# Row slot outermost in the 3x3 run's tiles, and the aggregation copied out of PSUM by ScalarE before VectorE adds it

## The chip, the core and the metric

The kernel runs on one core of a Trainium2 chip. The engines of the core work at the same time, each through its own list of instructions in order: PE (TensorE, the matmuls), DVE (VectorE), ACT (ScalarE), POOL (GpSimd) and SP (SyncE, which here only issues DMAs). They wait for one another with semaphores. The metric is the device time of the whole program in microseconds (us), lower is better. The kernel before took 6639.3 us, the median of 3 runs.

## The reference

The input is `x` of shape 8 x 32 x 128 x 128 (batch, channels, rows, columns). Two layers follow one another, each of the form x + layer(group-normalised x).

```python
xb = _patch_match_stack(x)             # per pixel: the 8 best of 25 shifts, 32 channels -> 256
dct = _conv(xb, dct_w, groups=C)
h = relu(_conv(_conv(xb, w1), w2, groups=CK, pad=1))    # 1x1 over 256 channels, then 3x3 per channel
h = relu(_conv(_conv(h, w3), w4, groups=CK, pad=1))
wiener = sigmoid(_conv(_conv(h, w5), w6, groups=CK, pad=1))
filt = _conv(wiener * dct, inv_dct_w, groups=C)
return _conv(filt, agg_w)              # 256 -> 32 channels, added to the residual x

x = x + layer0(_gn(x))
x = x + conv5x5(_gn(x))                # layer 1, per channel
```

The part that matters here is the chain of three pairs (a 1x1 convolution over 256 channels, then a 3x3 convolution of each channel by itself), and the last step of layer 0: `wiener * dct`, reduced from 256 to 32 channels (the aggregation) and added to `x`.

## The kernel before

**Tiling.** An image is worked in strips of R = 8 rows, 16 strips and a short one that flushes the pipeline, so 17 steps for each of the 8 images and 136 in all. The three pairs are a pipeline: in one step the loop `for i in (3, 2, 1, 0)` runs pair 3 of an older strip, pair 2 of a younger one, pair 1 of a still younger one, and with i = 0 the product with the DCT (`final_dct`). Each turn of that loop is called a slot; four slots make a step, and a step takes some 48 us.

**The 3x3 run.** The 256 channels are in two halves. The second half (128 channels) goes through `pointwise_v` (PE, then an ACT copy L678 into the tile `tv`) and `depthwise_v`: the first of the nine taps is an ACT instruction (L721), the other eight are DVE instructions (L724, "the taps") that accumulate in `acc`. The first half goes through PE alone: `pointwise_t` puts the 1x1 result through an ACT copy (L701) into the tile `t` of `tb`, whose 128 partitions are 4 rows x 32 channels. The free dimensions of `t` are, before the change, (channel group q, row slot, column): `[P, 4, 4, W]`. A 3x3 convolution of `t` on PE needs rows of two partition halves beside each other, so SP issues three DMAs from `t` to `t` for each strip and pair: L706 copies slots 2 and 3 of the lower 64 partitions to slots 0 and 1 of the upper 64, L708 copies slot 2 of the upper half to slot 1 of the lower, and L648 (`rows_before_t`) carries the last row over for the next strip. `depthwise_t` then runs the 3x3 taps as matmuls (L750) that read `t`, and ACT takes the result out of PSUM (L763). For pairs 1 and 3 these matmuls come in two parts, and the second waits for L706 and L708.

**The end of layer 0.** `final_dct` multiplies on DVE (L817). One slot later, in the slot with i = 3 of the next step, `final_add` runs as a generator in pieces, through the `later` of the main loop. Its first piece, after `pointwise_v`, is eight matmuls on PE into the PSUM tile `pa` (L830). Its second piece, in the middle of the slot, is the DVE addition `xr += pa` (L838), the DVE statistics of it (L839), and four DMAs on POOL that store `xr` to `x1d` (L843).

**What sets the order.** PE, DVE and ACT run exactly in the order in which the program emits their instructions (`manual_schedule`); the order on POOL and SP is planned by the framework. In each slot the emission is: `pointwise_v` and ACT's first tap; `final_add`'s first piece; for i = 0 the product; gather work of the next strips (`gather_select` on ACT, L616 and L617, twice a slot; `gather_load` DMAs on POOL, L602 for `ib`); `tick`, which puts background work of the next image on DVE (differences L444, searches L536 and L537, place numbers L551 to L560) within a budget; `final_add`'s second piece; the eight DVE taps; `pointwise_t` on PE with L701 on ACT; `gather_pixels` on PE (L631) with its ACT copy (L638); and the 3x3 matmuls of `t` left from the slot before. The PSUM tiles of `pa`, of both pointwise functions, of the gather and of the product share a ring of five banks (`ps_x`).

For a given pair the ring of the accumulators holds one tile for each half, so ACT's first tap L721 of pair 3 writes into the tile that the matmuls of `pa` have just read.

Of the kernel before, what the change touches and what calls it, by code (L numbers as in the profile page):

```python
# [8 lines left out]
F32 = mybir.dt.float32  # L9
# [7 lines left out]
P = 128  # L17
C, K, H, W = 32, 8, 128, 128
# [26 lines left out]
def bm3d_conv_preact(  # L45
# [16 lines left out]
    nc = tc.nc  # L62
# [5 lines left out]
    work = ctx.enter_context(tc.tile_pool(name="work", bufs=2))  # L68
# [48 lines left out]
    tb = [const.tile([P, 4, 4, W], F32, name=f"t{i}") for i in range(3)]  # L117
# [526 lines left out]
    def rows_before_t(i, b, n):  # L644

        t = tb[i - 1]
        if n < NS:
            nc.sync.dma_start(t[0:64, :, 0], t[64:P, :, 3])  # L648
        else:
            nc.gpsimd.memset(t[0:64, :, 0], 0.0)  # L650

    def rows_before_v(i, b, n):
        v = tv[i - 1]
# [26 lines left out]
    def pointwise_t(i, b, n, lhsT, src):  # L680
        t = tb[i - 1]
        nb = 2 if n < NS else 1
        nr = 4 if n < NS else i - 1
        if n == NS and i == 1:
            nc.gpsimd.memset(t[:, :, 2], 0.0)
        else:
            for q in range(2):
                ps = ps_x.tile([P, 2, 2, W], F32, name=f"p{i}_{b}_{n}_{q}", tag="x")
                for e in range(2):
                    s = slice(C * (2 * q + e), C * (2 * q + e + 1))  # L690
                    for g in range(2):
                        rows = src(g)
                        for r in range(nr):
                            nc.tensor.matmul(  # L694
                                ps[C * r : C * (r + 1), e, :nb],
                                lhsT[:, g, s],
                                rows[:, r : r + 4 * nb - 3 : 4],
                                start=g == 0,
                                stop=g == 1,
                            )  # L700
                nc.scalar.copy(  # L701
                    t[: C * nr, 2 * q : 2 * q + 2, 2 : 2 + nb], ps[: C * nr, :, :nb]
                )
            for r in range(i - 1) if n == 0 else range(i - 1, 4) if n == NS else ():
                nc.gpsimd.memset(t[C * r : C * (r + 1), :, 2], 0.0)
        nc.sync.dma_start(t[64:P, :, 0:nb], t[0:64, :, 2 : 2 + nb])  # L706
        if nb == 2:
            nc.sync.dma_start(t[0:64, :, 1], t[64:P, :, 2])  # L708

    def depthwise_v(i, b, n):  # L710
        v = tv[i - 1]
# [18 lines left out]
        rows_before_v(i, b, n)  # L730

    def depthwise_t(i, b, n):
        t = tb[i - 1].rearrange("p q (h k) w -> p q h k w", k=2)
        nb = 2 if n < NS else 1

        pt = [
            ps_dw.tile([P, 2, 2, W], F32, name=f"pw{i}_{b}_{n}_{u}", tag=f"dw{u}")
            for u in range(2)
        ]

        nh = [2 if n < NS else (i + 1 - u) // 2 for u in range(2)]

        parts = ((1, 2), (0, 1)) if i != 2 and n < NS else ((0, 2),)
        for ka, kz in parts:
            for u in range(2):
                hi, kz = 96 if u == 0 else P, min(kz, nh[u])
                for dx in (0, -1, 1):
                    xa, xz = max(0, -dx), min(W, W - dx)
                    for j in range(4 if kz > ka else 0):
                        nc.tensor.matmul(  # L750
                            pt[u][C * j : C * (j + 1), ka:kz, :nb, xa:xz],
                            dwd[0:hi, i - 1, u, j, dx + 1],
                            t[0:hi, j, ka:kz, :nb, xa + dx : xz + dx],
                            start=dx == 0,
                            stop=True,
                            skip_group_check=True,
                        )
        yield 1
        acc = accp.tile([P, R, W], F32, name=f"acc{i}_{b}_{n}_0", tag=f"acc{i}0")
        rows = acc.rearrange("p (k e) w -> p e k w", e=4)  # L760
        for u in range(2):
            if nh[u]:
                nc.scalar.activation(  # L763
                    rows[:, u : u + 2 * nh[u] - 1 : 2, :nb], pt[u][:, : nh[u], :nb], funcs[i - 1]
                )
        rows_before_t(i, b, n)
        accs[i, b, n][0] = acc

# [50 lines left out]
    def final_add(b, n, acc, xr, j0, j1):  # L819

        ya = R * n - 3 + j0
        whole = j1 - j0 == R
        nr, nw = (2, W) if whole else (j1 - j0, C)
        pa = ps_x.tile([P, 512], F32, name=f"pa_{b}_{n}", tag="x")
        pa = pa[:, : nr * nw].rearrange("p (r w) -> p r w", w=nw)
        for m in range(2):
            for j in range(4):
                ra = 2 * j if whole else j0
                xa = 0 if whole else C * j
                nc.tensor.matmul(  # L830
                    pa[C * j : C * (j + 1)],
                    lagg[:, m],
                    acc[m][:, ra : ra + nr, xa : xa + nw],
                    start=m == 0,
                    stop=m == 1,
                )
        yield
        nc.vector.tensor_add(xr, xr, pa)  # L838
        nc.vector.bn_stats(stats[b][:, n], xr)  # L839
        for j in range(4):  # L840
            ra = ya + 2 * j if whole else ya
            xa = 0 if whole else C * j
            nc.gpsimd.dma_start(  # L843
                x1d[b][:, ra : ra + nr, xa : xa + nw], xr[C * j : C * (j + 1)]
            )
# [184 lines left out]
    def until(cond, credit):  # L1030
        while not cond():
            turn(credit)

    with tc.manual_schedule(engines=ORDERED):
# [2 lines left out]
        push(mixes())  # L1037
        xbd[0] = dram.tile([P, 2, H, W], F32, name="xbd_0", tag="xbd")
        for i in range(3):
            nc.gpsimd.memset(tb[i][0:64, :, 0], 0.0)  # L1040
        for u in range(7):
            unit(gather_load, u)

# [8 lines left out]
        later = iter(())  # L1052

        for s in range(len(steps) + 2):
            if s < len(steps):
                b, n = steps[s]
                if s == 2:
                    push(bands())
                if n == (0 if b else 4) and b + 1 < NB:
                    until(lambda: b in ready, 4.0)  # L1060
                    push(prep(b + 1))
                if n == NS - 1 and b + 1 < NB:
                    until(lambda: b + 1 in ready, 4.0)
                    xbd[b + 1] = dram.tile([P, 2, H, W], F32, name=f"xbd_{b+1}", tag="xbd")
            for i in (3, 2, 1, 0):
                si = s - (i - 1 if i else 2)
                live = 0 <= si < len(steps)
                new_v = new_t = iter(())
                if live:
                    bi, ni = steps[si]  # L1070

                if live and i:
                    src = source(i, bi, ni)
                    pointwise_v(i, bi, ni, lws[i - 1], src)
                    new_v, new_t = depthwise_v(i, bi, ni), depthwise_t(i, bi, ni)
                    accs[i, bi, ni] = [None, next(new_v)]
                next(later, None)
                if live and not i:
                    if ni == 0:
                        x1d[bi] = dram.tile([C, H, W], F32, name=f"x1d_{bi}", tag="x1d")  # L1080
                        stats[bi] = work.tile([P, NS + 1, 6], F32, name=f"stat_{bi}", tag="stat")
                    xr, xf, j0, j1 = fins.pop(si)
                run("P")
                if live and not i:
                    final_dct(bi, ni, accs[3, bi, ni], xf, j0, j1)

                run("Q")
                if s < len(steps):
                    unit(gather_select, u + 1, (0,))
                    unit(gather_load, u + 3)  # L1090
                    tick(b, i)
                next(later, None)
                next(new_v, None)
                if live and i:
                    pointwise_t(i, bi, ni, lws[i - 1], src)
                next(kept, None)
                if s < len(steps):
                    unit(gather_pixels, u)
                next(dt, None)
                run("A")  # L1100
                next(dv, None)
                if s < len(steps):
                    unit(gather_select, u + 1, (1,))
                    u += 1
                next(dt, None)
                kept, dv, dt = dv, new_v, new_t
                if live and not i:
                    later = end(bi, ni, xr, j0, j1)
                if not i and 0 <= s - 1 < len(steps):
                    fins[s - 1] = final_load(*steps[s - 1])  # L1110
# [66 lines left out]
```

## Time and profile before

| What | Value |
|---|---|
| Median of 3 runs | 6639.3 us (6633.16 to 6649.49) |
| The profiled execution, its own time | 6645.45 us |
| Its span in the profile | 6643.7 us |
| Granted TensorE clock, mean | 0.978 |
| Busy share POOL | 46% |
| DMA: packets, bytes | 770751 packets, 886.20 MB |
| DMA t<-t on SP's queue | 792 of 128 KB, 384 of 256 KB |
| Share of the chain that ended last: PE, DVE, DMA, ACT | 43%, 29%, 9%, 8% |

Busy time is the sum of an engine's executing time; idle time is given ahead of a group of instructions with what ended it (the releaser). An engine that is busy 94% of the span leaves 6% for waits, and only waits of that engine, or of an engine that it then waits for, lengthen the program. A line such as "PE pw L750 <- DMA t<-t" means that PE stood idle before a matmul of line 750 until a DMA from `t` to `t` had landed.

### The profile page before, as it was taken

The numbers are of one execution on the slowest core, as the hardware profiler recorded it, in microseconds if no ns is written. First come the engines' busy times: TensorE is split into PE (matmuls) and PEld (weight loads), VectorE is DVE, ScalarE is ACT, GpSimd is POOL, SyncE is SP. The second block draws the span as 40 slices with busy tenths as digits, with TensorE's granted clock in tenths as the row PEclk, the third lists the DMA queues.
The fourth block names the chain that finished last, engine by engine and source line by source line (L and its number), as shares of the span: only waits on it lengthen the run. The fifth ranks groups of instructions, "written<-read, shape, count | busy, mean of one in ns | idle before, by whom it ended". The sixth has DMA issues, their size and how long they took to land.

```text
span 6643.7 us, 234197 instructions
## 1 busy us (share of the span) xinstructions
PE 6238.3 (94%) x102306; PEld 3236.5 (49%) x102306; DVE 5862.9 (88%) x8828; ACT 5054.4 (76%) x6698; POOL 3079.3 (46%) x5015
## 2 busy tenths in 40 slices
PE   5898899999999999999999999999999999999997
PEld 1444455544555545544555544554445544454553
DVE  7889988999889998898989998899888999887786
ACT  5787778777787777877778877887769777687772
POOL 8354346444464343643446444464435543344334
PEclk8899999999999999999999999999999999999998
DMA  4555555656555564655646656465555655556553
GB/s 85 126 138 130 131 131 130 148 134 140 131 143 136 130 147 118 149 134 133 144 121 147 147 126 149 120 154 136 130 137 132 148 136 130 125 141 145 137 133 82
DMA packets 770751, 886.20 MB, mean 133 GB/s; under 512 B 248880, under 2 KB 614000, under 8 KB 769728
## 3 DMA queue, kind: packets, MB, share of 16 engines
q0 software_dynamic: 383648, 611.87, 36.9%
q1 hardware_dynamic: 383568, 258.11, 17.6%
q8 instruction: 805, 13.19, 0.9%
q10 hardware_dynamic: 2512, 1.25, 0.1%
q14 instruction: 218, 1.79, 0.1%
HBM read 420.60 MB, written 216.49 MB: 96 GB/s over the span
## 4 chain that ended last, share of the span: by engine, by line
PE 43%; DVE 29%; DMA 9%; ACT 8%; POOL 6%; issue 4%; SPq 0%; ACTq 0%; DVEq 0%; POOLq 0%
DVE acc L724 20%; PE pw L750 14%; PE pv L670 11%; PE p L694 9%; PE pg L631 3%; DMA t<-t 3%; POOL xtd L424 2%; DVE df L444 2%; DVE idx L537 2%; PE pc L809 2%; ACT sel L616 2%; ACT df L452 2%; DMA xf<-xbd 2%; DVE acc L817 1%; PE p L923 1%
## 5 line engine op out<-in xcount | busy, mean ns | idle before, releaser
L724 DVE SCALAR_TENSOR_TENSOR acc<-tv,dwv,acc 128x1024 f32<-128x1024 f32 (+3 forms) x3264 | 4032.3, 1237 | 240.8 <-ACT acc L721 136.8
L750 PE MATMUL pw<-t,dwd 96*32 96x254 f32 (+7 forms) x31680 | 2124.6, 420 | 51.0 <-DMA t<-t 38.4
L750 PEld LDWEIGHTS pw<-t,dwd 96*32 96x32 f32 (+1 forms) x31680 | 1088.4, 110 | 874.5 <-issue 411.2
L616 ACT ACTIVATE sel<-ib,nplace 128x1024 f32<-128x1024 uint8 x1024 | 1172.1, 1145 | 37.4 <-DMA ib<-idxd 37.4
L617 ACT ACTIVATE sel<-sel 128x1024 f32<-128x1024 f32 x1024 | 1085.7, 1060 | 32.5
L694 PE MATMUL p<-acc,lw 128*32 128x256 f32 x16768 | 1002.9, 383 | 24.7 <-ACT tv L678 23.3
L670 PE MATMUL pv<-acc,lw 128*32 128x512 f32 x8448 | 956.2, 590 | 48.7 <-DVE acc L817 43.4
L602 POOL DMA_DIRECT2D ib<-idxd x512 | 292.5, 571 | 1241.8 <-ACT sel L616 1176.2
L790 POOL DMA_DIRECT2D xf<-xbd x1088 | 651.9, 631 | 316.1 <-PE pc L809 180.1
L694 PEld LDWEIGHTS p<-acc,lw 128*32 128x32 f32 x16768 | 579.2, 111 | 437.1 <-issue 79.4
L452 ACT ACTIVATE df<-df 128x786 f32<-128x786 f32 (+2 forms) x576 | 468.6, 861 | 340.5 <-DVE df L444 337.8
L631 PE MATMUL pg<-sel,xt 120*32 120x88 f32 (+1 forms) x24576 | 616.1, 244 | 63.6 <-ACT sel L617 50.7
L631 PEld LDWEIGHTS pg<-sel,xt 120*32 120x32 f32 x24576 | 556.8, 110 | 235.0 <-ACT sel L617 70.1
L678 ACT COPY tv<-pv 128x512 f32<-128x512 f32 (+2 forms) x784 | 437.1, 579 | 305.0 <-PE pv L670 293.0
L444 DVE TENSOR_TENSOR df<-xn 128x786 f32<-128x786 f32 (+2 forms) x576 | 531.6, 973 | 81.2 <-PE pd L459 80.2
L728 ACT ACTIVATE acc<-acc 128x1024 f32<-128x1024 f32 (+3 forms) x408 | 417.3, 1023 | 241.6 <-DVE acc L724 241.3
L763 ACT ACTIVATE acc<-pw 128x512 f32<-128x512 f32 (+2 forms) x808 | 438.5, 573 | 182.7 <-PE pw L750 182.0
L670 PEld LDWEIGHTS pv<-acc,lw 128*32 128x32 f32 x8448 | 286.0, 111 | 534.1 <-issue 428.7
L701 ACT COPY t<-p 128x512 f32<-128x512 f32 x800 | 424.4, 571 | 118.0 <-PE p L694 118.0
L721 ACT ACTIVATE acc<-tv,dwv 128x1024 f32<-128x1024 f32 (+3 forms) x408 | 454.9, 1115 | 33.9 <-PE pa L830 20.6
L670 PE MATMUL pv<-xb,lw 128*32 128x512 f32 x4096 | 473.5, 596 | 0.0
L694 PE MATMUL p<-xb,lw 128*32 128x256 f32 x8192 | 468.5, 379 | 1.0 <-DVE xy L935 0.9
(155 smaller groups left out, 5932.9 us busy)
## 6 DMA issues: line engine op xcount, KB each, us to landing
ib<-idxd POOLq DMA_DIRECT2D x512, 256.0 KB, 4.1
xbd<-xb POOLq DMA_DIRECT2D x128, 1024.0 KB, 5.9
xf<-xbd POOLq DMA_DIRECT2D x960, 128.0 KB, 7.1
t<-t SPq DMA_DIRECT2D x792, 128.0 KB
t<-t SPq DMA_DIRECT2D x384, 256.0 KB
tv<-tv SPq DMA_DIRECT2D x384, 130.0 KB
xt<-xtd POOLq DMA_DIRECT2D x240, 180.0 KB, 3.7
xtd<-xl POOLq DMA_DIRECT2D x192, 96.0 KB, 3.5
```

Of the source, the lines that this page charges most:

```text
L444: nc.vector.tensor_sub(df[:, :, ca:cz], xn[:, r0 : r0 + SR, ca:cz], xn[:, r0 + dy : r0 + dy + SR, ca + dx : cz + dx],)
L452: nc.scalar.activation(df[:, :, ca:cz], df[:, :, ca:cz], AF.Square)
L616: nc.scalar.activation(sel, ib, AF.Square, bias=nplace)
L617: nc.scalar.activation(sel, sel, AF.Relu, scale=-1.0, bias=1.0)
L631: nc.tensor.matmul(pg[C * j : C * (j + 1), :, :, xa:xz], xt[: 8 * QW, f * (NT // 2) + t], sels[j // 2][: 8 * QW, j % 2 * 2 : j % 2 * 2 + 2 ...
L670: nc.tensor.matmul(ps[C * j : C * (j + 1), :hr], lhsT[:, g, P + C * j : P + C * (j + 1)], src(g)[:, h : h + hr], start=g == 0, stop=g == 1,)
L694: nc.tensor.matmul(ps[C * r : C * (r + 1), e, :nb], lhsT[:, g, s], rows[:, r : r + 4 * nb - 3 : 4], start=g == 0, stop=g == 1,)
L721: nc.scalar.activation(acc, rows, AF.Copy, scale=tap)
L724: nc.vector.scalar_tensor_tensor(acc, rows, tap, acc, op0=ALU.mult, op1=ALU.add)
L750: nc.tensor.matmul(pt[u][C * j : C * (j + 1), ka:kz, :nb, xa:xz], dwd[0:hi, i - 1, u, j, dx + 1], t[0:hi, j, ka:kz, :nb, xa + dx : xz + dx ...
L763: nc.scalar.activation(rows[:, u : u + 2 * nh[u] - 1 : 2, :nb], pt[u][:, : nh[u], :nb], funcs[i - 1])
L790: nc.gpsimd.dma_start(xf[p : p + C, m, j0:j1], src[g, m, (h + m + 1) % 2, :, :, ya:yz])
```

## The change

The tile `t` keeps its size, but its free dimensions change places: (row slot, channel group, column) in place of (channel group, row slot, column). All users follow: the three DMAs of SP, the memsets, ACT's copy L701 (which now writes two runs apart for each slot) and the matmuls' reading pattern. For one partition, the rows that a DMA moves are now one run of 2 KB (one slot) or 4 KB (two slots), where they were four runs of 512 B or 1 KB. The bytes are the same.

In `final_add` ACT now copies `pa` from PSUM to a new SBUF tile `sums`, in the place where the DVE addition stood. The addition, the statistics and the four stores become a third piece, and the main loop calls it at the end of the slot, after the slot's DVE taps.

```diff
-            nc.sync.dma_start(t[0:64, :, 0], t[64:P, :, 3])
+            nc.sync.dma_start(t[0:64, 0], t[64:P, 3])
...
                 nc.scalar.copy(
-                    t[: C * nr, 2 * q : 2 * q + 2, 2 : 2 + nb], ps[: C * nr, :, :nb]
+                    t[: C * nr, 2 : 2 + nb, 2 * q : 2 * q + 2].rearrange("p b e w -> p e b w"),
+                    ps[: C * nr, :, :nb],
                 )
...
-        nc.sync.dma_start(t[64:P, :, 0:nb], t[0:64, :, 2 : 2 + nb])
+        nc.sync.dma_start(t[64:P, 0:nb], t[0:64, 2 : 2 + nb])
         if nb == 2:
-            nc.sync.dma_start(t[0:64, :, 1], t[64:P, :, 2])
+            nc.sync.dma_start(t[0:64, 1], t[64:P, 2])
...
     def depthwise_t(i, b, n):
-        t = tb[i - 1].rearrange("p q (h k) w -> p q h k w", k=2)
+        t = tb[i - 1].rearrange("p (h k) q w -> p q h k w", k=2)
...
         yield
-        nc.vector.tensor_add(xr, xr, pa)
+        sums = work.tile([P, 2 * W], F32, name=f"xs_{b}_{n}", tag="xs", bufs=1)
+        sums = sums[:, : nr * nw].rearrange("p (r w) -> p r w", w=nw)
+        nc.scalar.copy(sums, pa)
+        yield
+        nc.vector.tensor_add(xr, xr, sums)
         nc.vector.bn_stats(stats[b][:, n], xr)
...
                 next(dt, None)
+                next(later, None)
                 kept, dv, dt = dv, new_v, new_t
```

The sequences of PE's and of DVE's other instructions stay as they were: all that moves on DVE is the pair L838 and L839, from before the eight taps to after them.

More of the change, by code (lines that the diff above doesn't have):

```diff
@@ L647, in rows_before_t @@
         if n < NS:
-            nc.sync.dma_start(t[0:64, :, 0], t[64:P, :, 3])
+            nc.sync.dma_start(t[0:64, 0], t[64:P, 3])
         else:
-            nc.gpsimd.memset(t[0:64, :, 0], 0.0)
+            nc.gpsimd.memset(t[0:64, 0], 0.0)
     def rows_before_v(i, b, n):
@@ L684, in pointwise_t @@
         if n == NS and i == 1:
-            nc.gpsimd.memset(t[:, :, 2], 0.0)
+            nc.gpsimd.memset(t[:, 2], 0.0)
         else:
@@ L701, in pointwise_t @@
                 nc.scalar.copy(
-                    t[: C * nr, 2 * q : 2 * q + 2, 2 : 2 + nb], ps[: C * nr, :, :nb]
+                    t[: C * nr, 2 : 2 + nb, 2 * q : 2 * q + 2].rearrange("p b e w -> p e b w"),
+                    ps[: C * nr, :, :nb],
                 )
             for r in range(i - 1) if n == 0 else range(i - 1, 4) if n == NS else ():
-                nc.gpsimd.memset(t[C * r : C * (r + 1), :, 2], 0.0)
-        nc.sync.dma_start(t[64:P, :, 0:nb], t[0:64, :, 2 : 2 + nb])
+                nc.gpsimd.memset(t[C * r : C * (r + 1), 2], 0.0)
+        nc.sync.dma_start(t[64:P, 0:nb], t[0:64, 2 : 2 + nb])
         if nb == 2:
-            nc.sync.dma_start(t[0:64, :, 1], t[64:P, :, 2])
+            nc.sync.dma_start(t[0:64, 1], t[64:P, 2])
     def depthwise_v(i, b, n):
@@ L1039, in bm3d_conv_preact @@
         for i in range(3):
-            nc.gpsimd.memset(tb[i][0:64, :, 0], 0.0)
+            nc.gpsimd.memset(tb[i][0:64, 0], 0.0)
         for u in range(7):
```

## The prediction

> **What bounds the kernel now.** I read the page's busy times first, then the kernel in stretches, then the waits, then the timeline around the two places that change.
>
> ```profile
> PE 6238.3 (94%) x102306; PEld 3236.5 (49%) x102306; DVE 5862.9 (88%) x8828; ACT 5054.4 (76%) x6698; POOL 3079.3 (46%) x5015
> ...
> q0 software_dynamic: 383648, 611.87, 36.9%
> q1 hardware_dynamic: 383568, 258.11, 17.6%
> ```
>
> ```profile
> 1800.00:2610.00 810.00, 779.33 (x12870) 412.22 (x12874) 733.14 (x1101) 633.42 (x843) 383.75 (x626) 0.99 0.57 137
> 6224.00:6481.00 257.00, 257.00 (x4524) 132.29 (x4520) 204.13 (x181) 205.72 (x261) 80.33 (x147) 1.00 0.53 136
> ```
>
> The columns of the second view are the stretch, its length and the busy time of PE, weight loads, DVE, ACT and POOL. One image (1800 to 2610) keeps PE busy for 779 of 810 us, DVE for 733. In the last image, which prepares no next one, PE is busy all the time. So PE is the bound, and what can be won is its idle time: about 31 us for an image, 405 us in all (6643.7 less 6238.3), a good part of it at the start and the end. What ends these waits:
>
> ```profile
> DVE xr L838 <- PE pa L830: 237.1, 57, 9.9
> DVE acc L724 <- ACT acc L721: 136.8, 128, 4.7
> ACT acc L721 <- PE pa L830: 20.6, 62, 0.7
> PE pg L631 <- ACT sel L617: 50.7, 33, 2.3
> PE pv L670 <- DVE acc L817: 43.4, 25, 3.0
> PE pw L750 <- DMA t<-t: 38.4, 27, 4.0
> ```
>
> Total us, times, longest. The first line is the largest wait of DVE, and the change takes it away; the last is a wait of PE itself, which the new layout aims at.
>
> **Part 1, the addition.** Does removing the 237.1 us bring the taps forward? The timeline says no:
>
> ```profile
> 2044.86 0.42 DVE L838 TENSOR_TENSOR xr<-xr,pa 128x256 f32<-128x256 f32 x1 [3.25 <-PE pa L830]
> 2045.31 0.43 DVE L839 BATCH_NORM_STATS2 stat<-xr 128x6 f32<-128x256 f32 x1
> 2046.11 10.53 DVE L724 SCALAR_TENSOR_TENSOR acc<-tv,dwv,acc 128x1024 f32<-128x1024 f32 x8 [0.37 <-ACT acc L721]
> ```
>
> ```profile
> 2044.92 1.15 ACT L721 ACTIVATE acc<-tv,dwv 128x1024 f32<-128x1024 f32 x1 [0.34 <-PE pa L830]
> ```
>
> The taps need ACT's first tap L721, and L721 itself starts only when the matmuls of `pa` are done (it overwrites the accumulator that they read). It takes 1.15 us; the addition and the statistics fill 0.83 us of that, and DVE still waits 0.37. So in this kind of step the addition costs nothing today, and behind the taps it costs its 0.83 us. I went through all 136 additions in this way: in 62 DVE waits for `pa` (57 of them in the list above, the rest booked to DMAs that had landed long before), in 35 more it waits for a late L721 alone, and in 39 for neither. In the first 97 the taps start no earlier and 0.83 us of work moves behind them; in the 39 the order is merely swapped. The wait for `pa` turns into a wait for L721.
>
> Where does 0.83 us later on DVE hurt? Only where DVE stays without a gap until PE or ACT waits for it. In the image of 1835 to 2646 that holds after the additions at 2242.2, 2290.6 and 2343.0. The second:
>
> ```profile
> 2296.19 10.53 DVE L724 SCALAR_TENSOR_TENSOR acc<-tv,dwv,acc 128x1024 f32<-128x1024 f32 x8 [4.69 <-ACT acc L721]
> ```
>
> ```profile
> 2333.36 5.34 PE L670 MATMUL pv<-acc,lw 128*32 128x512 f32 x32 [2.93 <-DVE acc L817]
> ```
>
> From 2296 to the product (L817) DVE never rests, and PE then waits 2.93 us for it; it will wait 0.83 longer. After the others DVE meets a wait of its own first (8.4 us at 1885, 3.2 at 1937, the waits for `pa` between 2045 and 2243), which absorbs it. Three times 0.83, less a gap of 0.6 at 2391, is 1.9 us; times the 7 images that prepare a next one: +13 us. The new addition reads SBUF, which no row shows for this shape. Rows on both sides: 0.42 us from PSUM now, and 0.43 for three-operand work on 128x256 in SBUF (L557). I keep 0.42.
>
> The Trainium skill (SBUF — State Buffer, Who interferes with whom) says that a VectorE instruction with two SBUF inputs contends with GpSimd instructions that read SBUF. All GpSimd compute rows after the start here are memsets, which read nothing, so by that rule the term stays as it is.
>
> ACT's copy is new: 136 of 128x256 or less from PSUM. The nearest rows are copies of that shape, 374 ns (L678) and 389 (L298): 136 x 0.37 = 50 us of ACT time. It adds no wait, since L721 ahead of it has waited for `pa`. Queued behind it is L701, which mostly waits for PE anyway (118.0 us over 105 of 800). It counts where ACT is full: the step from 1835 to 1889 (ACT busy 53 of 54 us) and the one from 2291, so 2 x 0.37 x 7 = +5 us; bounds 0 and 50. `pa`'s bank comes free some 2 to 3 us later, five allocations ahead of its next use: 0.
>
> The four stores leave later by the taps, 10.5 us. On POOL's planned order they pass two or three issues, mostly a gather load (L602, L591), which thereby leaves earlier; behind them stand loads of `xr` and `xf`, used a step later, and the next `ib`. In that image an `ib` whose issue would be put off has 10 us or more until its use: 0. If that cover fails, ACT waits for `ib` (37.4 us in 7 waits now).
>
> **Part 2, the layout.** Per page, a q1 packet takes 48.8 ns at 673 B on average (17.6% of 16 x 6643.7 us over the packets), a q0 packet 102 ns at 1595 B: about 10 ns + 0.058 ns per byte. A t<-t of 128 KB alone goes from 256 packets of 39 ns to 64 of 128 ns: over 16 engines 0.63 to 0.51 us. Unhindered the change gives 0.1 us. But PE's waits arise where it is hindered:
>
> ```profile
> 2017.71 6.08 POOL L937 DMA_DIRECT2D out_dram<-xy  x4 [5.04 <-DVE xy L935]
> ...
> 2022.53 1.98 SPq L708 DMA_DIRECT2D t<-t  x1
> ...
> 2034.61 1.93 PE L750 MATMUL pw<-t,dwd 96*32 96x256 f32 x16 [2.60 <-DMA t<-t]
> ```
>
> Here L708 needs 12 us beside the output stores, where its median is 4.35 (from the sixteen semaphore increments of each). On a contested engine the 32 packets of L706 and L708 take turns with the stores'; 8 larger ones need a quarter of the turns. The waits average 1.4 us, so a landing 3 us earlier ends nearly all. Not all of it is won: where DVE soon sets the pace, PE waits there instead. I took of each of the 27 waits no more than DVE's own waiting at the next addition (the wait at 2034.6: 2.60, of 3.6; that at 1621.5: none): 24 us of the 38.4. Bounds: 2 x 0.1 x 27 = 5 us, and 38.4 plus a 3.1 us wait for `tv` behind them, 41 us; larger packets could hold up a neighbour, by a few us. I take 24, which the wait rows are nearest to. Memsets, L701 (571 ns; L763, written in the same two-part pattern, 573) and PE's reads (254 columns in two runs 382 ns, 256 in one 384) cost 0.
>
> A rule speaks against this: the Trainium skill (DMA: Bandwidth & Descriptors, Why small descriptors are slow (HBM only)) holds that transfers from SBUF to SBUF don't suffer from small descriptors. By it the 24 would be near 0.
>
> **Sum.** -24 + 13 + 5 = -6 us on the profiled execution's own 6645.45 us: 6639. That execution is 6 us above the median of the runs, 6639.3, so by the median 6633.
>
> **Rivals.** *Faster*: the landings come early and both costs drown, since DVE also gains in the 39 steps where the taps start 0.7 us earlier: -35 us or so, 6604. For it: the image without background work has PE at 100%. Against it: PE's waits for L817 and L560. *Slower, DVE becomes the bound*: the 0.83 us counts in ten of the 17 steps of an image, 10 x 0.83 x 7 = 58, with 5 for ACT and 24 won: +39, 6678. It decides once DVE's gaps (77 us an image) lie behind PE's waits instead of ahead. For it: DVE at 733 of 810. Against it: the gaps listed above. *The layout does nothing*: L708 waits for whole runs of store packets whatever its own count: +18 - 5 = +13, 6652; for it, the packets of L708 end when the stores do.
>
> **Chances.** No change (0.3%, 20 us, is about what a measurement tells from none: 6619 to 6659) 0.37, own range 6614 to 6652; faster rival 0.32; DVE rival 0.17; idle layout 0.14, half of it above 6659. Faster 0.32 + 0.06 of the first's lower edge = 0.38; slower 0.17 + 0.07 + 0.04 = 0.28; same 0.34. The range 6595 to 6682 leaves out the full 41 without costs, and ACT's 50 us in full.
>
> **What would show it.** "DVE xr <- PE pa" gone and "DVE acc <- ACT acc" (136.8) up by about 60 x 0.8 = 50 us or more: part 1 as read. "PE pw <- DMA t<-t" below 10 us: part 2. "PE pv <- DVE acc L817" up from 43.4 by about 13. I am wrong if DVE's wait for L721 doesn't grow, if L708 still needs 12 us beside the stores, or if ACT comes to wait for `ib`.

## The result, and the profile after

The changed kernel is slower: 6697.7 us median of 4 runs (6685.89 to 6701.66) against 6642.06 us for the kernel before, run beside it. The ratio is 1.0076, with an interval of [1.0061, 1.0091], so some +50 us. The forecast was no change, 6633 us, with a range up to 6682.

The page of the changed kernel, busy times and the DMA queues (lines of the addition have moved by 5, the taps are now L725, the first tap L722, the product L818, ACT's copy L841, the addition L843):

```profile
PE 6249.4 (93%) x102306; PEld 3220.2 (48%) x102306; DVE 5855.4 (87%) x8828; ACT 5086.9 (76%) x6834; POOL 3075.7 (46%) x5015
...
q1 hardware_dynamic: 157776, 258.11, 16.1%
```

PE does the same matmuls, so its idle time tells most of the story: 6699.5 less 6249.4 is 450 us, 45 more than before; its busy time grew by 11 us. The packets of SP's queue fell from 383568 to 157776 as the layout meant them to, and ACT has 136 instructions more. Now the waits of the changed kernel (total us, times, longest):

```profile
DVE acc L725 <- ACT acc L722: 457.5, 125, 10.5
...
PE pv L670 <- DVE acc L818: 47.7, 26, 2.4
...
PE pw L751 <- DMA t<-t: 32.2, 20, 3.8
...
ACT acc L722 <- PE pa L831: 18.9, 55, 1.1
...
PE pv L670 <- ACT xs L841: 17.1, 18, 1.6
...
PE pc L810 <- DVE acc L818: 16.1, 11, 2.0
```

VectorE's wait for `pa` is gone, but the wait for ACT's first tap went from 136.8 to 457.5 us: the taps start no earlier. PE's waits for DVE's product (L818) grew from 43.4 and 3.8 to 47.7 and 16.1. A wait that was not there before is `pv <- ACT xs`: `pv` takes the PSUM bank that `pa` held until ACT's copy. And PE still waits 32.2 us for transfers of `t`, where the forecast had them below 10.

### The profile page after: what moved, and what is told of

The parts are those of the page before. It is cut to its first block, busy times and chain, and to the rows that moved or that the text cites. A ratio compares the mean times of both kernels' runs of the same rounds, so it can differ in the third digit from the quotient of the medians.

```text
span 6699.5 us, 234454 instructions
## 1 busy us (share of the span) xinstructions
PE 6249.4 (93%) x102306; PEld 3220.2 (48%) x102306; DVE 5855.4 (87%) x8828; ACT 5086.9 (76%) x6834; POOL 3075.7 (46%) x5015
## 3 DMA queue, kind: packets, MB, share of 16 engines
q1 hardware_dynamic: 157776, 258.11, 16.1%
## 4 chain that ended last, share of the span: by engine, by line
PE 26%; DVE 25%; DMA 6%; ACT 6%; POOL 4%; issue 4%; DVEq 0%; SPq 0%; POOLq 0%; ACTq 0%
DVE acc L725 18%; PE pw L751 9%; PE pv L670 7%; PE p L694 6%; PE pg L631 2%; POOL xtd L424 2%; DMA xf<-xbd 2%; DMA t<-t 1%; DVE idx L537 1%; DVE df L444 1%; DMA out_dram<-xy 1%; PE pc L810 1%; DVE acc L818 1%; ACT sel L616 1%; ACT df L452 1%
## 5 line engine op out<-in xcount | busy, mean ns | idle before, releaser
L725 DVE SCALAR_TENSOR_TENSOR acc<-tv,dwv,acc 128x1024 f32<-128x1024 f32 (+3 forms) x3264 | 4034.0, 1237 | 562.4 <-ACT acc L722 457.5
L751 PE MATMUL pw<-t,dwd 96*32 96x254 f32 (+7 forms) x31680 | 2129.5, 420 | 45.5 <-DMA t<-t 32.2
L616 ACT ACTIVATE sel<-ib,nplace 128x1024 f32<-128x1024 uint8 x1024 | 1173.7, 1146 | 35.7 <-DMA ib<-idxd 35.7
L670 PE MATMUL pv<-acc,lw 128*32 128x512 f32 x8448 | 962.6, 592 | 65.0 <-DVE acc L818 47.7
L848 POOL DMA_DIRECT2D x1d<-xr x544 | 276.1, 514 | 620.3 <-DVE xr L843 553.4
L701 ACT COPY t<-p 128x512 f32<-128x512 f32 x800 | 425.6, 574 | 104.9 <-PE p L694 104.3
L722 ACT ACTIVATE acc<-tv,dwv 128x1024 f32<-128x1024 f32 (+3 forms) x408 | 455.0, 1115 | 32.6 <-PE pa L831 18.9
```

What stands on the lines that cost most here:

```text
L616: nc.scalar.activation(sel, ib, AF.Square, bias=nplace)
L670: nc.tensor.matmul(ps[C * j : C * (j + 1), :hr], lhsT[:, g, P + C * j : P + C * (j + 1)], src(g)[:, h : h + hr], start=g == 0, stop=g == 1,)
L722: nc.scalar.activation(acc, rows, AF.Copy, scale=tap)
L725: nc.vector.scalar_tensor_tensor(acc, rows, tap, acc, op0=ALU.mult, op1=ALU.add)
L751: nc.tensor.matmul(pt[u][C * j : C * (j + 1), ka:kz, :nb, xa:xz], dwd[0:hi, i - 1, u, j, dx + 1], t[0:hi, j, ka:kz, :nb, xa + dx : xz + dx ...
```

## The experiments

Every ratio below is against the kernel before, run beside it, with its 95% interval.

**The two halves apart.** First the layout of `t` alone, with the addition as before:

> The kernel before with the new layout of t alone; additions as before. Theory A (the moved addition and the copy are the loss, the layout is idle): ratio 0.996 to 1.001, PE's wait for t<-t down from 38.4 us by no more than 15. Rival B (the longer packets crowd out other transfers and are the loss): 1.005 to 1.008. The forecast's own pricing of this part, -24 us: 0.9964.

Measured: 0.9978 [0.9967, 0.9989], some -15 us. Then the addition's half alone, with the old layout:

> The old layout, with the ACT copy and the late addition. Theory A: all of the loss is here, ratio 1.007 to 1.010. Rival B: 0.999 to 1.003. The forecast's own pricing, +18 us: 1.0027.

Measured: 1.0098 [1.0080, 1.0115], some +65 us. So the layout helps, a little less than forecast, and the loss is all in the addition's half, where the forecast had +18 us.

**Where ACT's copy stands.** With the old layout, once the copy and the addition both in the middle of the slot, once the copy directly behind ACT's first tap and the addition late:

```diff
         yield
-        nc.vector.tensor_add(xr, xr, pa)
+        sums = ...
+        nc.scalar.copy(sums, pa)
+        nc.vector.tensor_add(xr, xr, sums)
```

> The old layout; ACT copies the aggregation to SBUF in the middle of the slot, and VectorE adds it there too, at its old place. If the copy itself (47 us of ACT time, and PSUM held until ACT gets to it) is the loss: ratio 1.004 to 1.008, with PE's wait for ACT's copy near 17 us. If the later place of VectorE's addition is the loss: 1.000 to 1.002. VectorE now waits for the copy behind two gather selections of ACT, which may cost it more than the wait for PE did.

Measured: 1.0330 [1.0311, 1.0348]; both theories missed. The waits of that kernel say why:

```profile
DVE xr L841 <- ACT xs L840: 622.9, 109, 11.7
```

In the middle of the slot ACT has gather work queued ahead of the copy, and VectorE, which runs in order, stands behind it with its taps. So the copy and the late addition belong together: with the copy in the middle of the slot, the addition can't stay there. The early copy, against the kernel with the addition's half alone:

```diff
-        yield
         sums = ...
         nc.scalar.copy(sums, pa)
+        yield
         yield
         nc.vector.tensor_add(xr, xr, sums)
```

> The old layout; ACT's copy stands directly behind its first tap, ahead of the gather selections, so the PSUM bank comes free some 2 to 3 us earlier; VectorE's addition stays at the end of the slot. If the held bank is half of the loss: ratio 1.002 to 1.005 where add_only has 1.008, and PE no longer waits for the copy. If VectorE's later place is the loss: the same ratio as add_only.

Measured: 1.0073 [1.0056, 1.0090], some 17 us below the 1.0098 of the late copy, with intervals that overlap. The wait of `pv` for the copy (13.3 us there) is gone in its trace, and PE's wait for `t<-t` is smaller as well (43.7 us, 57.4 there), so which of the two won the 17 us can't be told here. Most of the loss stays.

**The bank, and the stores.** The addition late but straight from PSUM, without a copy:

> The old layout, no ACT copy: VectorE adds straight from PSUM at the end of the slot, so pa's bank is held until then; statistics and stores are late too, and SP's planned order is the same as in the kernel with the late addition alone (1.0098). Theory A (SP's order): 1.007 to 1.012. Theory B (ACT's copy and what it delays): 1.000 to 1.005. Theory C (late stores): 1.006 to 1.012. A longer hold of the bank may add up to 0.006 under each.

Measured: 1.0184 [1.0169, 1.0198], just past the upper end of what the theories A and C allow with a longer hold of the bank (1.018), and far above B. Now `pa`'s bank is held until the end of the slot, and one wait shows a part of the price:

```profile
PE pv L670 <- DVE xr L839: 19.7, 6, 3.5
```

So the copy is worth its place if the addition is to be late. Then the four stores alone, moved to the end of the slot:

```diff
         nc.vector.tensor_add(xr, xr, pa)
         nc.vector.bn_stats(stats[b][:, n], xr)
+        yield
         for j in range(4):
```

> The kernel before with one thing moved: the four x1d stores are emitted at the end of the slot, the addition and the statistics stay in the middle and read PSUM. SP's planned order is that of the kernel before. Theory A (SP's order carries the loss): 0.998 to 1.002. Theory B (ACT's copy): 0.998 to 1.002. Theory C (late stores): 1.004 to 1.010.

Measured: 0.9987 [0.9978, 0.9996]. The late stores cost nothing; theory C falls.

**SP's order.** SP's queue is planned by the framework, and it plans anew when the order of the other engines changes (the late stores alone left it as it was). Two stretches of SP and PE at the start of an image's steps, before and after, show what that can do. Columns: start, duration, engine and line. Before:

```profile
1169.35 0.59 SPq L706 DMA_DIRECT2D t<-t  x1
1169.98 0.62 SPq L708 DMA_DIRECT2D t<-t  x1
1171.01 0.59 SPq L648 DMA_DIRECT2D t<-t  x1
1172.46 0.50 SPq L655 DMA_DIRECT2D tv<-tv  x1
```

After:

```profile
1169.66 1.05 ACT L701 COPY t<-p 128x512 f32<-128x512 f32 x2
...
1170.30 0.46 SPq L648 DMA_DIRECT2D t<-t  x1
...
1174.08 0.48 SPq L655 DMA_DIRECT2D tv<-tv  x1
...
1174.98 0.46 SPq L707 DMA_DIRECT2D t<-t  x1
...
1175.50 0.58 SPq L709 DMA_DIRECT2D t<-t  x1
...
1176.77 2.75 PE L751 MATMUL pw<-t,dwd 96*32 96x256 f32 x46
...
1183.17 5.32 PE L751 MATMUL pw<-t,dwd 96*32 96x256 f32 x48 [3.65 <-DMA t<-t]
```

L707 and L709 need only ACT's copy L701, which ends at 1170.71. But they now stand behind L655, which waits on other work until 1174.08, and leave more than 4 us late; PE then stalls 3.65 us. It is a matter of place more than of number: over the whole run, 23 of the two kinds of transfer (L706 and L708) leave over 2 us after the last ACT copy ahead of them before the change and 24 after it, only other ones (without the seven of the short strips, which need no such copy and now leave some 17 us after one). To undo this alone, the transfers are chained in the order of the kernel before:

```diff
+        for ch in SP_ORDER:
...
+            if prev is not None:
+                tc.add_manual_dep(dma.ins, prev.ins.name, ..., reason="order")
+            prev = dma
```

> The changed kernel with one thing undone: the order of the four kinds of t and tv transfers on SP's queue, which the framework planned anew in it (74 of 1560 places differ from the kernel before, some 27 transfers of t moved behind a tv transfer that waits), is held to that of the kernel before. The changed kernel stood at 1.0076. Theory A (the new order on SP carries a good part of the loss: transfers of t are issued up to 5 us later, and PE stalls of over 3 us follow): ratio 0.999 to 1.004, and PE's wait for t<-t falls from 32.2 us below 20. Theory B (ACT's copy, which holds pa's bank and ACT's time, carries it): 1.006 to 1.009. Theory C (the late stores on POOL carry it, with the next image's loads behind them): 1.006 to 1.009. The forecast's own pricing (nothing on SP): as the changed kernel.

Measured: 1.0048 [1.0036, 1.0060], against 1.0076 for the changed kernel: SP's order carries some 0.28%, 19 us [6, 31]. PE's wait for `t<-t` is 21.2 us (32.2). It is a part, less than theory A had. With the copy early as well:

> The changed kernel with two things undone: SP's order of the t and tv transfers held to that of the kernel before (with that alone 1.0048), and ACT's copy of pa put directly behind its first tap, so that pa's bank comes free early. What is left of the change: the new layout, a copy on ACT, and the addition, statistics and stores at the end of the slot. Theory A (SP's order, pa's bank, and DVE's 0.83 us behind the taps each carry a part): 1.000 to 1.0035, PE's wait for ACT's copy of pa gone (18.4 us with the order alone held). Theory B (the bank carries nothing; DVE's late addition or ACT's 50 us carry the rest): 1.004 to 1.006.

Measured: 1.0051 [1.0034, 1.0068]. The wait of `pv` for the copy is gone, and the time is the same. So with SP's order held the bank carries nothing that could be measured; what early_copy won over the late copy may have been how its transfers fell.

**DVE or ACT?** An unused copy of `pa` on ACT, with the addition in its old place and SP's order held:

> The kernel before with SP's order held, and ACT's copy of pa (behind its first tap) added without use: VectorE still adds from PSUM in the middle of the slot. It shows what the 46 us of ACT time cost alone. The forecast's term: +5 us, 1.0008. Theory A (ACT has room, the loss is elsewhere): 0.999 to 1.002. Theory B (ACT's time is the rest of the loss): 1.004 to 1.008.

Measured: 1.0061 [1.0044, 1.0079]. That looked like ACT's time, but the waits said otherwise:

```profile
DVE xr L862 <- ACT xs L860: 419.7, 95, 13.5
```

In the built program the addition, which reads the same PSUM tile as the copy, waits for the copy though it uses nothing of it. So this kernel also puts the addition between ACT's first tap and DVE's taps. The statistics alone moved late:

> The kernel before with SP's order held, and the statistics (0.43 us of DVE) and the stores moved to the end of the slot; the addition stays in the middle. The late stores alone stood at 0.9987. It moves half of the 0.83 us of DVE that the change moves behind the taps. The forecast's term for all of it was +13 us: half is 1.001. Theory A (DVE's late work carries most of what is left, some 20 to 30 us): 1.001 to 1.003. Theory B (the bank and ACT carry it): 0.998 to 1.001.

Measured: 1.0020 [1.0009, 1.0030], some 13 us for half of DVE's 0.83 us (the late stores are in it). Then the two cleanly apart. ACT's time alone, with a copy that reads a constant:

```diff
         yield
+        sums = ...
+        nc.scalar.copy(sums, still...)
         nc.vector.tensor_add(xr, xr, pa)
```

> The kernel before with SP's order held, and on ACT a copy of a constant SBUF tile of pa's size, unused, in the place of the change's copy. VectorE adds from PSUM as before and waits for nothing new; only ACT's time is added. The forecast's term: +5 us, 1.0008. Theory A (ACT's time passes on nearly in full, 46 us): 1.004 to 1.007. Theory B (the 1.0061 of the unused copy of pa came from the addition waiting for it, ACT has room): 0.999 to 1.002.

Measured: 0.9997 [0.9987, 1.0006]. And DVE's late work alone, with no copy and with `pa`'s bank free (the addition reads the constant in place of `pa`, so this kernel leaves the aggregation out of its output):

```diff
         yield
-        nc.vector.tensor_add(xr, xr, pa)
+        yield
+        nc.vector.tensor_add(xr, xr, still...)
```

> SP's order held, no copy on ACT; VectorE's addition, statistics and stores at the end of the slot, and the addition takes a constant SBUF tile in place of pa, so that pa's bank is free as soon as it is written. The aggregation's sum is thereby left out of the output. Only DVE's order is changed (and the stores, which alone cost nothing). The forecast's term: +13 us, 1.002. Theory A (0.83 us behind the taps at each strip costs more than the forecast had): 1.003 to 1.006. Theory B (DVE has room; ACT carries the loss): 0.999 to 1.002.

Measured: 1.0061 [1.0045, 1.0077], some +41 us. This is the bulk of the loss: the copy's ACT time (51 us with the constant, 46 in the changed kernel) cost nothing that could be measured, and 0.83 us of DVE for each strip, moved behind the taps, cost 41 us. Where they do can be read from the steps, from one strip's matmuls of `pa` to the next. The table is the mean over images 1 to 6 of how much longer a step is (us) than in the mean of three kernels of about equal time (before, act_alone, stores_late), each of which lies within 0.5 of that mean in every step, and up to 0.9 from another:

```
step          0     1     2     4     5     6     7     8    13    all 17
late_alone  +0.7  +0.7  +0.2   0.0  +2.2  +0.8  +0.9  +0.1  +0.5   +7.1
after       +3.6  -1.5  +1.2  +0.4  +2.5  +0.8  +0.3  +0.1  +0.5   +9.6
after_pin   +0.8  -1.2  +1.6  +0.5  +3.0  +0.8  +1.0  +0.6  +0.5   +6.8
```

The +3.6 of step 0 is SP's order (+0.8 when it is held). With the late addition alone, step 6 is longer by 0.7 or 0.8 in each of the six images and step 5 by 0.9 to 3.4, while steps 0 and 1 range from -2.2 to 5.0, so that their +0.7 are not told from scatter. The largest entry that all share is step 5. In image 2 that is the step from 2190.3; first DVE in the kernel before, then DVE and PE with the late addition alone, and PE's clock behind the wait (0.50; the columns of this row are named in the last section):

```profile
2219.32 10.52 DVE L724 SCALAR_TENSOR_TENSOR acc<-tv,dwv,acc 128x1024 f32<-128x1024 f32 x8
2229.76 1.27 DVE L817 TENSOR_TENSOR acc<-acc,pc 128x512 f32<-128x512 f32 x2
2231.62 1.28 DVE L817 TENSOR_TENSOR acc<-acc,pc 128x512 f32<-128x512 f32 x2 [0.58 <-PE pc L809]
...
2242.18 0.42 DVE L838 TENSOR_TENSOR xr<-xr,pa 128x256 f32<-128x256 f32 x1 [2.85 <-PE pa L830]
```

```profile
2221.20 10.52 DVE L745 SCALAR_TENSOR_TENSOR acc<-tv,dwv,acc 128x1024 f32<-128x1024 f32 x8
2231.63 1.28 DVE L838 TENSOR_TENSOR acc<-acc,pc 128x512 f32<-128x512 f32 x2
2233.82 1.29 DVE L838 TENSOR_TENSOR acc<-acc,pc 128x512 f32<-128x512 f32 x2 [0.91 <-PE pc L830]
```

```profile
2232.36 1.43 PE L830 MATMUL pc<-xf,ldct 64*64 64x512 f32 x6 [1.70 <-DVE acc L838]
```

```profile
2233.00:2236.40 3.40, 3.40 (x66) 2.22 (x64) 2.58 (x4) 0.68 (x2) 0.00 (x0) 0.50 0.02 5
```

Counted from the step's start (2190.31 and 2189.78), DVE's first product starts, at the end of its run of taps, at 39.45 us before and at 41.85 with the late addition. Of these 2.4 us the addition is 0.83. The other 1.6 are there at the start of the step, where the first run of taps begins at 2.6 us before and at 4.2 with the late addition: just ahead of it PE waits 1.75 us for `t<-t` before and only 0.16 there, so PE enters the step earlier than ACT and DVE do. Before, the product just freed the bank in time for PE's next `pc`; DVE even waited 0.58 us for PE. Now PE waits 1.70 us for DVE, and runs at half clock for 3.4 us soon after, which is another 1.7 us of work not done: 3.4 of the 4.0 us by which this step is longer (54.7 against 50.7). The 2.85 us in which DVE waited for `pa` before lie behind this place. Image 2 is the largest difference; over the six images the product starts 39.3 to 41.1 us into the step before and 41.4 to 41.9 with the late addition. The clock falls in three of the six (2, 5 and 6), where the step is 3.1 to 3.4 us longer than the mean of the three kernels; in the others it is 0.9 to 1.2.

**Why is the first tap late?** The forecast said that it overwrites the accumulator that `pa`'s matmuls read. With two buffers for that accumulator:

```diff
-        out_ = accp.tile([P, R, W], ..., tag=f"acc{i}1")
+        out_ = accp.tile([P, R, W], ..., tag=f"acc{i}1", bufs=2 if i == 3 else 1)
```

> The changed kernel with SP's order held (1.0048) and two buffers for pair 3's accumulator of the second half, so that ACT's first tap no longer waits for pa's matmuls. The forecast said that the first tap is late because it overwrites what they read. If so: VectorE's wait for the first tap falls from 445 us to below 300, and the ratio to 1.000 to 1.003. If ACT is late by itself (its copies of pv ahead of the tap wait for PE): that wait stays above 400 us and the ratio within 1.0035 to 1.006.

Measured: 1.0047 [1.0033, 1.0062], as with one buffer. The waits of that kernel:

```profile
DVE acc L748 <- ACT acc L745: 439.7, 120, 12.2
...
ACT tv L699 <- PE pv L691: 296.1, 333, 1.4
```

The first tap no longer waits for `pa`, and DVE waits for it as long as ever (445.2 us with one buffer). So ACT comes to it late by itself. Its copies of `pv`, which stand ahead of the tap, wait 296 us for PE in all slots together; that they are what makes it late is likely, not shown.

**The output stores.** The forecast took it that `t`'s transfers are held up by output stores. Each of them moves 62 partitions; here it is split:

```diff
-                for a, z in ((0, 62), (66, P)):
+                for a, z in ((0, 48), (48, 62), (66, 114), (114, P)):
```

> The new layout of t alone, and each output store of 62 partitions split into one of 48 and one of 14. The layout alone stood at 0.9978. The forecast took it that t's transfers are late because output stores of 2 KB packets stand ahead of them on few DMA engines. If that is what delays them and the split spreads the stores: 0.992 to 0.997, PE's wait for t<-t below 10 us (17.7 with the layout alone). If not, or if the extra DMAs on POOL cost as much: 0.997 to 1.003.

Measured: 0.9940 [0.9927, 0.9953], PE's wait for `t<-t` 12.0 us (below 10 was expected). And with the old layout:

> The kernel before with the output stores of 62 partitions split into 48 and 14, old layout. The layout alone stood at 0.9978, both at 0.9940. If the two gains are separate: 0.995 to 0.9975. If the split does it all and the layout adds nothing beside it: 0.993 to 0.995. If the split helps only small numbers of large packets (the new layout): 0.998 to 1.001.

Measured: 0.9941 [0.9927, 0.9955], 6607 us: a gain of 39 us, and the new layout adds nothing to it. The DMA lists of the kernel before and of the one with split stores (KB each, median us to landing):

```profile
out_dram<-xy POOLq DMA_DIRECT2D x112, 124.0 KB, 11.0
```

```profile
out_dram<-xy POOLq DMA_DIRECT2D x112, 96.0 KB, 2.5
out_dram<-xy POOLq DMA_DIRECT2D x112, 28.0 KB, 2.4
```

The store of 62 partitions lands after 11.0 us; its two parts after 2.5 and 2.4. PE's wait for `t<-t` is 13.4 us with the split (38.4 before). Of the 384 transfers of L708, 29 are under way together with an output store before: these land after 11.2 us (median), the other 355 after 4.2. With the new layout alone it is 9.9 us for 30, with the split alone 5.3 for 15. With the new layout, and late stores of `x1d` on top:

> New layout (alone 0.9978), split output stores (with the layout 0.9940) and late stores of x1d (alone 0.9987); addition and statistics as in the kernel before, SP's order too. If the gains add: 0.9915 to 0.9940. If late stores only moved noise: 0.9930 to 0.9955. Slower than 0.996 if they collide on POOL.

Measured: 0.9942 [0.9926, 0.9958]: nothing more. Last, the changed kernel with split stores, once with SP's new order and once with the old:

> The changed kernel with the output stores split (in the kernel before the split gave 0.9941, with or without the new layout). The late addition alone cost 0.0061, SP's new order 0.0028. If the parts are separate: 0.9941 + 0.0061 + 0.0028 = 1.003, so 1.001 to 1.005. If the split also takes away what SP's order costs, since t's transfers then land sooner: 0.998 to 1.001.

Measured: 1.0038 [1.0025, 1.0052].

> The same with SP's order held to that of the kernel before. If the late addition is all that is left: 0.9941 + 0.0061 = 1.000, so 0.998 to 1.002. If it is within 0.001 of the run with the new order, that order costs nothing beside split stores; if it is 0.002 to 0.004 below it, the order costs as much as with the whole stores.

Measured: 1.0030 [1.0019, 1.0041], above the expected range. SP's order is then worth 0.0008, with intervals that overlap. The copy and the late addition cost 0.90% here, from 0.9940 with the split and the new layout. With whole stores the same pair, from layout_only to after_pin, costs 0.70%. The difference of 0.20% is within the intervals of these four runs (some 0.24%), so they don't show that the parts fail to add up.

## Why the prediction was wrong

The terms beside each other, in us (ratios times some 6645 us; intervals in brackets):

| Step of the forecast | Forecast | Measured |
|---|---|---|
| 0.83 us of DVE behind the taps | +13 | +41 [30, 51] (late_alone, the stores in it) |
| ACT's copy | +5 | -2 [-9, +4] (act_alone) |
| `pa`'s bank free later | 0 | 17 us between add_only and early_copy (intervals overlap), none with SP's order held |
| stores later on POOL | 0 | -9 [-15, -3] (stores_late) |
| SP's order | not in the sum | +19 [6, 31] (after less after_pin) |
| layout of `t` | -24 | -15 [-22, -7] (layout_only) |
| Sum | -6 | 41 - 2 + 19 - 15 = +43; the changed kernel: +50 [40, 60] |

**The step that failed** is "Where does 0.83 us later on DVE hurt?" The three additions that the forecast named, at 2242.2, 2290.6 and 2343.0, are the starts of steps 6, 7 and 8, and they came out well: 1.9 us forecast, 0.8 + 0.9 + 0.1 measured. The failure is the sentence after them, that behind the other additions DVE "meets a wait of its own first", among them "the waits for `pa` between 2045 and 2243". The test was for DVE's next wait, wherever it came. In step 5 that wait comes 10 us after the product on which PE depends, so PE is delayed first, and by a product that had only just been in time. The forecast read this off one image (1835 to 2646) and counted it seven times. At the same place of image 4 PE already waited for that product in the kernel before (in image 5 as well, 0.87 us), so the cover was used up there:

```profile
3843.84 1.08 PE L809 MATMUL pc<-xf,ldct 64*64 64x512 f32 x6 [1.21 <-DVE acc L817]
```

Steps 0, 1, 5 and 13, which the forecast held covered, come to 4.1 us of an image's 7.1, of which the 2.2 of step 5 are clear of the scatter. In step 6 DVE's lateness passes on at its own size, and in step 7 in the mean; in step 5 it grows in half of the images, since PE loses 1.7 us of clock after the stall, which no term of the forecast had.

**What was left out** is SP. The forecast moved the stores past their neighbours on POOL and priced that rightly at nothing. But it asked of SP's queue only what the layout does to it. In the changed kernel 74 of its 1560 transfers of `t` and `tv` stand elsewhere, which could be read from the built program before any run.

**What was right.** The wait for `pa` turned into a wait for the first tap (136.8 to 457.5 us; "by 50 or more" was asked), so nothing of the 237.1 us was won. But the reason given beside it, that the tap overwrites the accumulator, carries next to nothing: it is a wait of 20.6 us in all before, and taking it away (ring2) won nothing. PE's waits for the product grew by 16.6 us (about 13 was forecast), though 12.3 of them before `pc` and not before `pv`. ACT's 46 us cost nothing (+5 was forecast, with two misreadings: L701, which "mostly waits for PE anyway", does so in 105 of 800, and in the step from 2291, called full, ACT is busy for 38.5 of 52 us), and its waits for `ib` did not grow (35.7 us, 37.4 before). The new addition takes 402 ns in the mean (400 before), so no contention of shared SBUF reads shows here. That `pa`'s bank comes free later "at 0" is half right: the trace has 17.1 us of PE waiting for it, but taking them away won nothing once SP's order was held.

**The layout's term** had the right sign and place and was too large. The forecast expected landings 3 us earlier where output stores stand beside them; with the layout alone L708's median there went from 11.2 to 9.9 us, 1.3 earlier, and its sign of being wrong came true: one beside the stores at 2019.2 still took 12.6 us. PE's wait fell from 38.4 to 17.7 us, not below 10, and a gain of 15 us came of it. The Trainium skill (DMA: Bandwidth & Descriptors, Why small descriptors are slow (HBM only)) was weighed against it, with a gain near 0 by that rule. The measured gain lies between the two, outside 0; and with split stores, where the transfers are hindered less, it is 0. The cause that the forecast named, output stores beside the transfers, is borne out by the split.

**The rivals.** The one in which DVE becomes the bound (58 us of DVE, 6678 us, 0.17) had the mechanism and nearly the size: it took 0.83 us in 10 steps of each image, where the runs show 2.2 us in one step and 0.5 to 0.9 in five others, two of them within the scatter. That its sum comes so near is luck in part: DVE's share was too large by 17 us, and SP's 19 us were not in it.

## What to carry to other kernels

Work moved to a later place on an engine is covered by a wait only if that wait comes before the next thing that another engine needs from it; follow the engine to its next product, not to its next idle time. When a step is moved, compare the built order of every queue that a planner fills, also of those that the step does not use. And where transfers land late, look at what stands beside them: here splitting one store gave 39 us, more than making the late transfers themselves cheaper.

## What was not expected of the hardware

**A stall costs more than its length.** In the changed kernel, PE's granted clock before and behind the 3.65 us stall at 1183 (stretch, length, busy time of PE, weight loads, DVE, ACT and POOL, the clock, DMA share, GB/s):

```profile
1176.80:1179.50 2.70, 2.70 (x53) 1.98 (x44) 2.70 (x4) 2.67 (x4) 1.78 (x3) 1.00 1.05 225
1183.20:1188.40 5.20, 5.20 (x52) 2.84 (x56) 4.76 (x18) 0.60 (x1) 2.25 (x4) 0.50 1.00 308
```

After the stall the clock is 0.50, and 52 matmuls take 5.20 us where 53 took 2.70. Of the 48 such stretches in that trace's clock records, 32 are 3.4 us long and 9 are 6.8. Not every stall has one behind it: in after_pin PE waits 2.03 us for the product in step 5 of images 1, 2, 3, 4 and 6, and the clock falls after it in 3, 4 and 6 only. What decides is not shown here. The sum of the stretches is 290 us before, 298 in the changed kernel, 312 with the late addition alone, 343 with the addition's half alone and 403 in copy_mid, and 269 with split stores.

**62 partitions in one store.** 124 KB in 62 partitions took 11.0 us to land, 96 KB in 48 took 2.5. The cut changed more than the number of partitions: the queue of the stores has 31488 packets of 32 bytes before and 4608 with the split, 210 fewer for each of its 128 stores of this kind, and POOL's issue of one store took 1.52 us where each part takes 0.59. How the packets are shared among the DMA engines is not in these traces, and other cuts were not tried, so which of this makes the store slow is open.
